# Weighted context of a perceiver layer: fifteen products of thirds of the channels for three blocks of tokens, in place of seven products of halves for two

## The chip, the core and the metric

The kernel runs on one core of one Trainium2 chip. A core has a matrix engine (TensorE, "PE" in the profile; "PEld" is its weight load), a vector engine (VectorE, "DVE"), a scalar engine (ScalarE, "ACT"), GpSimd ("POOL") and a queue engine that only issues transfers ("SP"). The metric is the device time of one execution in microseconds; the median of several runs counts. All data are 32-bit floats.

## The reference, cut to what matters

The layer has three parts: a cross attention of 256 tokens `x` over 25,088 context tokens, a small self attention, and a mixture of experts. The change touches only the cross attention:

```python
# x: 256 x 512 after a layer norm; ctx: 25088 x 512
qp = q @ Wq.T + bq                     # 256 x 128
kp = ctx @ Wk.T + bk                   # 25088 x 128
vp = ctx @ Wv.T + bv                   # 25088 x 512
z = sigmoid(qp @ kp.T / sqrt(128))     # 256 x 25088
x = x + z @ vp
```

There is no softmax, so `z @ vp = (z @ ctx) @ Wv.T + rowsum(z) * bv`. The kernel computes the weighted context `z @ ctx` (256 x 512) first and projects it once at the end.

## The kernel before

**Blocks and groups.** The context is cut into blocks of 128 tokens and groups of J = 4 blocks, so there are G = 49 groups of 512 tokens. For each group four things are done:

1. The keys need the context with channels on the partitions. `turn(g)` (line 313) does this with one VectorE transpose of a second copy of the group ("quarters", loaded by `load_quarters`, line 108, in four transfers of 256 KB); for the first two groups, `turn_by_pe` (line 320) does it on TensorE, 16 transposes each, with copies out of PSUM by ScalarE and VectorE.
2. `keys(g)` (line 339): four matmuls of 512 columns, then a VectorE instruction that adds the bias and moves the result out of PSUM.
3. `scores(g)` (line 360): four matmuls of 256 columns into two PSUM banks, each followed by a ScalarE sigmoid of 512 elements. The result `zT` has 128 tokens on the partitions and, for each block, 256 queries.
4. `values(g)` (line 432): the weighted context. It is a product of a matrix of 2 x 2 pieces (two halves of the queries, two blocks of tokens) and one of 2 x 2 pieces (two blocks of tokens, two halves of the channels). Written out, that is eight products of pieces. The kernel uses the known scheme with seven, which takes sums of pieces as operands: `query_sums` (line 412) makes four sums of `zT` and `context_sums` (line 421) four sums of the context, all on VectorE. The seven products are accumulated over all groups in seven half banks of PSUM (`xacc`), and combined once at the end. A group holds two pairs of blocks, so it makes 14 matmuls of 256 columns.

`summed(g)` (line 384) adds `zT` into `zsum` on VectorE, for the row sums of `z`.

**Order.** Instructions passed to `in_turn` keep their order in the program on their engine. The loop, per group g: loads for g + 2; scores(g); query sums of g; keys(g + 1); channel sums of g + 1; turn(g + 2); summed(g); values(g). TensorE therefore runs scores, keys of the next group, and products, in this order. `in_group` names the groups after which weights of later stages are fetched, each held back by a small GpSimd copy.

**Buffers.** PSUM has eight banks: three in rotation and one apart for keys, scores and transposes (`bank`, line 80), four for the products (`pacc`). In SBUF there are four context groups, three groups of quarters, and two buffers each of turned groups (`cT`), query sums (`S`) and channel sums (`T`); `zT` has three.

**Before the loop:** layer norm of `x`, its transposes, `turn_by_pe(0)`, the query projection, the first keys, `turn_by_pe(1)`. **After the loop:** eight VectorE instructions (lines 501 to 508) combine the seven products into `zc`, `turn_zc` (line 515) turns it in four parts, and the value projection follows (`py`, line 564). The rest of the kernel is the self attention and the experts.

Of the kernel before, what the change touches and what calls it, by code (L numbers as in the profile page):

```python
# [21 lines left out]
def tile_perceiver_layer(  # L22
# [39 lines left out]
    J = 4  # L62
    G = S // (J * P)
    NE = INNER // P
    TOPK = 8

# [10 lines left out]
    psum = ctx.enter_context(tc.tile_pool(name="psum", bufs=3, space=bass.MemoryType.PSUM))  # L77
    turns = [0]

    def bank(name):  # L80
        turns[0] += 1
        return apart(name) if turns[0] % 4 == 0 else among_three(name)

    def among_three(name):
        return psum.tile([P, 512], F32, tag="one", name=name)

    def apart(name):
        return psum.tile([P, 512], F32, tag="apart", name=name, bufs=1)

    pacc = cross.enter_context(tc.tile_pool(name="pacc", bufs=4, space=bass.MemoryType.PSUM))  # L90
# [3 lines left out]
    def load(name, shape, src, pool=const):  # L94
        t = pool.tile(shape, F32, tag=name, name=name, bufs=1)
        nc.sync.dma_start(t, src)
        return t
# [9 lines left out]

    def load_quarters(g):

        q = cpool.tile([P, J * P // R, D // NA], F32, tag="quarters", name=f"quarters_{g}", bufs=3)  # L110
        group = context[g * J * P : (g + 1) * J * P, :]
        for a in range(NA):
            nc.sync.dma_start(
                q[a * R : (a + 1) * R, :, :],
                group.rearrange("(b i) (a d) -> a i b d", i=R, a=NA)[a],
            )
        quarter_tiles[g] = q

    def load_context(g, parts=1):
        t = cpool.tile([P, J, D], F32, tag="ctx", name=f"ctx_{g}", bufs=4)  # L120
        group = context[g * J * P : (g + 1) * J * P, :].rearrange("(j p) d -> p j d", j=J)
        n = J // parts
        for j in range(0, J, n):
            nc.sync.dma_start(t[:, j : j + n, :], group[:, j : j + n, :])
        ctx_tiles[g] = t


    BY_PE = 2
    bk_sb = const.tile([QK, 1], F32, tag="bk", name="bk")
    nc.scalar.dma_start(bk_sb, bk)  # L130
    bq_sb = const.tile([QK, 1], F32, tag="bq", name="bq")
    nc.scalar.dma_start(bq_sb, bq)
    x_sb = act.tile([P, NT, D], F32, tag="x", name="x_sb")
    for t in range(NT):
        nc.sync.dma_start(x_sb[:, t, :], x[t * P : (t + 1) * P, :])
    wqT_sb = load("wqT", [P, ND, QK], rows(wqT))
    load_context(0, parts=J)
    wk_plain_sb = load("wk_plain", [P, ND, QK], rows(wkT), cpool)
    load_context(1)
    wkT_sb = const.tile([P, ND, QK], F32, tag="wkT", name="wkT_sb")  # L140
    for a in range(NA):
        nc.sync.dma_start(
            wkT_sb[a * R : (a + 1) * R, :, :],
            wkT.rearrange("(a c r) e -> a r c e", a=NA, r=R)[a],
        )

# [13 lines left out]
    def all_of(src):  # L160
# [25 lines left out]
        4: [fetch_wv, fetch_bv],  # L186
        6: [fetch_aq],
        8: [fetch_akv, fetch_lng, fetch_lnb],
        10: [fetch_aout],
        12: [fetch_lnog, fetch_lnob, fetch_gates],  # L190
# [42 lines left out]
    idle_sb = cpool.tile([P, 4, 512], F32, tag="T", name="idle_sb")[:, 0, :]  # L233
    nc.vector.memset(idle_sb, 0.0)

    def keep_warm(n):
        pi = bank("pi")
        for _ in range(n):
            nc.tensor.matmul(pi, lhsT=idle_sb[:, 0:P], rhs=idle_sb, start=True, stop=True)
# [60 lines left out]
    def transposed(dst, src, nm):  # L300

        for c in range(ND):
            pt = bank(f"pt_{nm}_{c}")
            for t in range(NT):
                nc.tensor.transpose(
                    pt[:, t * P : (t + 1) * P], src[:, t, c * P : (c + 1) * P], ident
                )
            nc.vector.tensor_copy(dst[:, c, :], pt[:, :T])


    turned_tiles = {}

    def turn(g):

        cT = cpool.tile([P, ND, J * P // R, R], F32, tag="cT", name=f"cT_{g}")
        q = quarter_tiles.pop(g)
        in_turn(nc.vector.transpose(cT, q.rearrange("p b (c r) -> p c b r", r=R)))  # L317
        turned_tiles[g] = cT

    def turn_by_pe(g):  # L320

        cT = cpool.tile([P, ND, J * P // R, R], F32, tag="cT", name=f"cT_{g}")
        ct = ctx_tiles[g]
        for c in range(ND):
            pt = bank(f"ptc_{g}_{c}")
            for j in range(J):
                in_turn(
                    nc.tensor.transpose(
                        pt[:, j * P : (j + 1) * P], ct[:, j, c * P : (c + 1) * P], ident
                    )  # L330
                )
            to = cT[:, c, :, :].rearrange("p b r -> p (b r)")
            if c % 2:
                nc.scalar.copy(to, pt)
            else:
                in_turn(nc.vector.tensor_copy(to, pt))
        turned_tiles[g] = cT

    def keys(g):

        cT = turned_tiles.pop(g)
        pk = bank(f"pk_{g}")
        w = wk_plain_sb if g < BY_PE else wkT_sb
        for c in range(ND):
# [4 lines left out]
                    rhs=cT[:, c, :, :].rearrange("p b r -> p (b r)"),  # L349
# [5 lines left out]
        in_turn(nc.vector.tensor_scalar(kT, pk, bk_sb, None, ALU.add))  # L355
        return kT

    zsum = cpool.tile([P, J, T], F32, tag="zsum", name="zsum", bufs=1)

    def scores(g, kT):  # L360

        zT = cpool.tile([P, J, T], F32, tag="zT", name=f"zT_{g}", bufs=3)
        for h in range(J // 2):
            pz = bank(f"pz_{g}_{h}")
            for i in range(2):
                j = 2 * h + i
                in_turn(
                    nc.tensor.matmul(  # L368
                        pz[:, i * T : (i + 1) * T],
                        lhsT=kT[:, j * P : (j + 1) * P],  # L370
                        rhs=qT,
                        start=True,
                        stop=True,
                    )
                )
            nc.scalar.activation(  # L376
                zT[:, 2 * h : 2 * h + 2, :].rearrange("p j t -> p (j t)"),
                pz,
# [3 lines left out]
        return zT  # L382

    def summed(g, zT):
        if g == 0:
            in_turn(nc.vector.tensor_copy(zsum, zT))
        else:
            in_turn(nc.vector.tensor_add(zsum, zsum, zT))  # L388
# [6 lines left out]
    NP = J // 2  # L395
    HD = D // 2
    product = {}
    for i, names in enumerate((("00", "01"), ("2", "3"), ("1",), ("4", "11"))):
        held = pacc.tile([P, 512], F32, tag="acc", name=f"xacc_{i}")
        for k, nm in enumerate(names):  # L400
            product[nm] = held[:, k * HD : (k + 1) * HD]
    sums, channel_sums = {}, {}

    def z_of(zT, i, b):

        i = 1 - i
        return zT[:, b::2, i * P : (i + 1) * P]

    def c_of(ct, b, k):

        return ct[:, b::2, k * HD : (k + 1) * HD]

    def query_sums(g, zT):
        s = cpool.tile([P, 4, NP, P], F32, tag="S", name=f"S_{g}")
        s1, s2, s3, s4 = (s[:, i, :, :] for i in range(4))
        in_turn(nc.vector.tensor_add(s1, z_of(zT, 1, 0), z_of(zT, 1, 1)))  # L416
        in_turn(nc.vector.tensor_sub(s2, s1, z_of(zT, 0, 0)))
        in_turn(nc.vector.tensor_sub(s3, z_of(zT, 0, 0), z_of(zT, 1, 0)))
        in_turn(nc.vector.tensor_sub(s4, z_of(zT, 0, 1), s2))
        sums[g] = s1, s2, s3, s4  # L420

    def context_sums(g):
        ct = ctx_tiles[g]
        s = cpool.tile([P, 4, NP, HD], F32, tag="T", name=f"T_{g}")
        t1, t2, t3, t4 = (s[:, i, :, :] for i in range(4))
        in_turn(nc.vector.tensor_sub(t1, c_of(ct, 0, 1), c_of(ct, 0, 0)))
        in_turn(nc.vector.tensor_sub(t2, c_of(ct, 1, 1), t1))  # L427
        in_turn(nc.vector.tensor_sub(t3, c_of(ct, 1, 1), c_of(ct, 0, 1)))  # L428
        in_turn(nc.vector.tensor_sub(t4, t2, c_of(ct, 1, 0)))  # L429
        channel_sums[g] = t1, t2, t3, t4  # L430

    def values(g, zT):
        ct = ctx_tiles.pop(g)
        s1, s2, s3, s4 = sums.pop(g)
        t1, t2, t3, t4 = channel_sums.pop(g)
        for nm, lhs, rhs in (
            ("00", z_of(zT, 0, 0), c_of(ct, 0, 0)),
            ("01", z_of(zT, 0, 1), c_of(ct, 1, 0)),
            ("2", s2, t2),
            ("3", s3, t3),  # L440
            ("1", s1, t1),
            ("4", s4, c_of(ct, 1, 1)),
            ("11", z_of(zT, 1, 1), t4),
        ):
            for p in range(NP):

                in_turn(
                    nc.tensor.matmul(  # L448
                        product[nm],
                        lhsT=lhs[:, p, :],  # L450
                        rhs=rhs[:, p, :],
                        start=(g == 0 and p == 0 and nm in ("00", "2", "1", "4")),
# [925 lines left out]
```

## Time and profile before

| | us |
|---|---|
| median of 3 runs | 798.08 (797.95 to 798.08) |
| profiled execution, its own time | 798.27 |
| span of that execution | 796.4 |
| loop: first scores start | 18.02 |
| last product of the loop starts, for a run of 1.03 | 563.21 |
| value projection starts | 565.75 |

A profile shows one execution. For each engine it gives the busy time, and for groups of equal instructions the line of the code, what is written and read, the shape, the count, the busy time, the mean duration of one in ns, and the idle time before them with what ended it. A matmul of 32-bit floats appears as two instructions, so 14 matmuls of the code are 28 in the profile. Matmuls overlap in the engine: the duration of one (380 ns for 256 columns) is longer than the distance between the starts of two. The weight loads' starts show the distance best.

```profile
L346 PE MATMUL pk<-cT,wkT_sb 128*128 128x512 f32 x376 | 169.0, 592 | 0.0
L448 PE MATMUL xacc<-T,S 128*128 128x256 f32 x588 | 134.9, 379 | 0.0
L317 DVE STREAM_TRANSPOSE cT<-quarters 128x2048 f32<-128x2048 f32 x47 | 108.3, 2304 | 0.0
ctx<-in_context SPq DMA_DIRECT2D x48, 1024.0 KB, 6.5
quarters<-in_context SPq DMA_DIRECT2D x188, 256.0 KB, 8.4
```

The first three lines are groups of instructions, the last two transfers (count, size of each, microseconds from issue to landing).

### The profile page before, as it was taken

To read this page: it belongs to the slowest core of one execution; us is meant where nothing else is said; L and a number is where in the kernel's file an instruction comes from. 1 tells how busy PE (TensorE), PEld (TensorE's weight loads), DVE (VectorE), ACT (ScalarE), POOL (GpSimd) and SP (SyncE) were. 2 spreads that over 40 slices of the span, in tenths; PEclk is the share of its full clock that TensorE was granted. 3 is DMA by queue.
4 is the path that set the end of the run, shared out by engine and by line. 5 is a ranking of instruction groups with operands and counts; after the bars stand their busy time and mean duration, and the time that the engine had idled before them with its cause. 6 is when DMAs were issued, how large, how long until landed. Compare 5 with 4: busy or idle time off the path is not lost.

```text
span 796.4 us, 8701 instructions
## 1 busy us (share of the span) xinstructions
PE 784.4 (98%) x3298; PEld 564.5 (71%) x3298; DVE 496.6 (62%) x820; ACT 112.3 (14%) x248; POOL 21.4 (3%) x44
## 2 busy tenths in 40 slices
PE   9999999999999999999999999999999899999996
PEld 5777777777777777777777777777676586776563
DVE  5766776677766776677766776676656563512222
ACT  2111101110011101110011101110245220110110
POOL 1000000000000000000000000000223000000000
PEclk9999999999999999999999999999999999999998
DMA  9967998999887778777887778720510042769400
GB/s 279 257 165 185 258 243 242 244 248 242 200 205 185 174 176 209 191 184 170 197 206 184 174 177 211 193 72 0 196 44 1 1 133 96 252 233 392 163 1 30
DMA packets 150497, 139.59 MB, mean 175 GB/s; under 512 B 7984, under 2 KB 109872, under 8 KB 150448
## 3 DMA queue, kind: packets, MB, share of 16 engines
q1 hardware_dynamic: 150160, 138.96, 67.1%
q8 instruction: 28, 0.46, 0.3%
q14 instruction: 21, 0.17, 0.1%
q10 hardware_dynamic: 288, 0.00, 0.0%
HBM read 138.42 MB, written 0.52 MB: 174 GB/s over the span
## 4 chain that ended last, share of the span: by engine, by line
PE 96%; DVE 2%; ACT 1%; DMA 0%; POOL 0%; issue 0%; ACTq 0%
PE xacc L448 37%; PE pk L346 21%; PE pz L368 11%; PE ph_e L936 7%; PE pd_e L983 3%; PE ph_s L936 3%; PE pd_s L983 2%; PE pa L651 2%; PE ph_few L1205 1%; PE pw L715 1%; PE py L564 1%; PE ps L741 1%; PE ptp L792 1%; PE po_few L1236 1%; PE pf L1182 1%; PE pd_few L1250 1%
## 5 line engine op out<-in xcount | busy, mean ns | idle before, releaser
L346 PE MATMUL pk<-cT,wkT_sb 128*128 128x512 f32 x376 | 169.0, 592 | 0.0
L448 PE MATMUL xacc<-T,S 128*128 128x256 f32 x588 | 134.9, 379 | 0.0
L376 ACT ACTIVATE zT<-pz 128x512 f32<-128x512 f32 x98 | 58.3, 597 | 479.9 <-PE pz L368 479.2
L448 PEld LDWEIGHTS xacc<-T,S 128*128 128x128 f32 x588 | 111.7, 190 | 15.2
L346 PEld LDWEIGHTS pk<-cT,wkT_sb 128*128 128x128 f32 x376 | 71.4, 190 | 69.9 <-issue 67.4
L317 DVE STREAM_TRANSPOSE cT<-quarters 128x2048 f32<-128x2048 f32 x47 | 108.3, 2304 | 0.0
L448 PEld LDWEIGHTS xacc<-ctx,zT 128*128 128x128 f32 x392 | 74.3, 190 | 31.3 <-issue 23.0
L448 PE MATMUL xacc<-ctx,zT 128*128 128x256 f32 x392 | 93.0, 380 | 0.1
L368 PE MATMUL pz<-qT,kT 128*128 128x256 f32 x392 | 92.6, 379 | 0.0
L368 PEld LDWEIGHTS pz<-qT,kT 128*128 128x128 f32 x392 | 74.4, 190 | 10.1
L416 DVE TENSOR_TENSOR S<-zT 128x256 f32<-128x256 f32 x49 | 20.8, 425 | 91.4 <-ACT zT L376 91.4
L355 DVE TENSOR_SCALAR kT<-pk,bk 128x512 f32<-128x512 f32 x49 | 36.8, 751 | 59.8 <-PE pk L346 59.8
L936 PE MATMUL ph_e<-fT,gu 128*128 128x256 f32 x256 | 57.4, 381 | 0.0
L388 DVE TENSOR_TENSOR zsum<-zsum,zT 128x1024 f32<-128x1024 f32 x48 | 56.8, 1184 | 0.0
L936 PEld LDWEIGHTS ph_e<-fT,gu 128*128 128x128 f32 x256 | 48.0, 190 | 10.6 <-issue 2.2
L448 PE MATMUL xacc<-T,zT 128*128 128x256 f32 x196 | 50.3, 379 | 0.0
L448 PE MATMUL xacc<-ctx,S 128*128 128x256 f32 x196 | 50.3, 379 | 0.0
L448 PEld LDWEIGHTS xacc<-T,zT 128*128 128x128 f32 x196 | 37.2, 190 | 5.1
L448 PEld LDWEIGHTS xacc<-ctx,S 128*128 128x128 f32 x196 | 37.2, 190 | 5.1
L427 DVE TENSOR_TENSOR T<-ctx,T 128x512 f32<-128x512 f32 x49 | 33.9, 692 | 1.7
L428 DVE TENSOR_TENSOR T<-ctx 128x512 f32<-128x512 f32 x49 | 33.5, 685 | 0.0
L429 DVE TENSOR_TENSOR T<-T,ctx 128x512 f32<-128x512 f32 x49 | 33.5, 684 | 0.0
(231 smaller groups left out, 611.3 us busy)
## 6 DMA issues: line engine op xcount, KB each, us to landing
ctx<-in_context SPq DMA_DIRECT2D x48, 1024.0 KB, 6.5
quarters<-in_context SPq DMA_DIRECT2D x188, 256.0 KB, 8.4
gu<-in_e_gate_up SPq DMA_DIRECT2D x12, 1024.0 KB, 7.5
dn<-in_e_down SPq DMA_DIRECT2D x11, 512.0 KB, 4.7
gu_s<-in_s_gate_up SPq DMA_DIRECT2D x8, 512.0 KB, 5.9
a_wqT<-in_a_wqT SPq DMA_DIRECT2D x1, 2048.0 KB, 8.8
a_wout<-in_a_woutT SPq DMA_DIRECT2D x1, 2048.0 KB, 9.9
dn_s<-in_s_down SPq DMA_DIRECT2D x4, 512.0 KB, 7.2
```

Source lines behind the costliest of these rows:

```text
L317: in_turn(nc.vector.transpose(cT, q.rearrange("p b (c r) -> p c b r", r=R)))
L346: nc.tensor.matmul(pk, lhsT=w[:, c, :], rhs=cT[:, c, :, :].rearrange("p b r -> p (b r)"), start=(c == 0), stop=(c == ND - 1),)
L355: in_turn(nc.vector.tensor_scalar(kT, pk, bk_sb, None, ALU.add))
L368: nc.tensor.matmul(pz[:, i * T : (i + 1) * T], lhsT=kT[:, j * P : (j + 1) * P], rhs=qT, start=True, stop=True,)
L376: nc.scalar.activation(zT[:, 2 * h : 2 * h + 2, :].rearrange("p j t -> p (j t)"), pz, AF.Sigmoid, scale=1.0 / math.sqrt(QK),)
L388: in_turn(nc.vector.tensor_add(zsum, zsum, zT))
L427: in_turn(nc.vector.tensor_sub(t2, c_of(ct, 1, 1), t1))
L428: in_turn(nc.vector.tensor_sub(t3, c_of(ct, 1, 1), c_of(ct, 0, 1)))
L429: in_turn(nc.vector.tensor_sub(t4, t2, c_of(ct, 1, 0)))
L448: nc.tensor.matmul(product[nm], lhsT=lhs[:, p, :], rhs=rhs[:, p, :], start=(g == 0 and p == 0 and nm in ("00", "2", "1", "4")), stop=(g == ...
L936: nc.tensor.matmul(ph[:, f * T + lo : f * T + hi], lhsT=gu[:, c, col : col + P], rhs=fT[:, c, lo:hi], start=(c == 0), stop=(c == ND - 1),)
L983: nc.tensor.matmul(pd, lhsT=hT[:, f, t * P : (t + 1) * P], rhs=dn[:, f, :], start=(f == 0), stop=(f == NI - 1),)
```

## The change

- **Groups of three blocks.** J is 3. 25,088 tokens are 65 groups of 384 and one block over; that block becomes group 0 (`blocks_of`, `tokens_of`), and is the only one turned by TensorE (four transposes).
- **Fifteen products.** The pieces are now two halves of the queries by three blocks of tokens, and three blocks of tokens by three thirds of the channels. Written out, that is 18 products; the change uses a scheme with fifteen. 512 channels do not divide by three, so the thirds are 170 to 172 wide and overlap. `a02` is the first half of the queries with the third block, `b21` the third block with the second third, `s` are sums of a's, `t` sums of b's, `p` the products. Ten query sums of 128 elements are made by VectorE; of thirteen channel sums of 172 elements six by VectorE and seven by GpSimd. The products fill six PSUM banks. In the first group, which has only its middle block, three sums and six products are left.
- **Banks.** Keys and scores have one bank each (`keys_bank`, `scores_bank`), the products six. The scores of a group come in two parts, of two blocks and of one, through the same bank.
- **Order.** The products run one group late: scores of two blocks of g; four products of g - 1; scores of the third block; keys(g + 1); the other eleven products of g - 1. VectorE: channel sums of g, query sums of g, turn(g + 2). GpSimd: channel sums of g, then `summed(g)`. Loads are issued three groups ahead, with five context buffers.
- **Engines.** The bias of the keys is added by ScalarE, `zsum` by GpSimd.
- **Start.** The two halves of `x` are loaded on two queues, the query weights on ScalarE's queue, the biases on GpSimd's; the two layer norms are interleaved; three pairs of warming matmuls in place of four.
- **End.** ScalarE copies five of the six product banks to SBUF, 21 sums on VectorE and GpSimd combine them, `zc` is turned in two parts, the second between the matmuls of the first projection.

```diff
-    J = 4
-    G = S // (J * P)
+    J = 3
+    HEAD = S % (J * P)
+    G = 1 + S // (J * P)
...
-    pacc = cross.enter_context(tc.tile_pool(name="pacc", bufs=4, space=bass.MemoryType.PSUM))
+    psum = ctx.enter_context(tc.tile_pool(name="psum", bufs=1, space=bass.MemoryType.PSUM))
+    pacc = cross.enter_context(tc.tile_pool(name="pacc", bufs=6, space=bass.MemoryType.PSUM))
...
     def keys(g):
...
-        in_turn(nc.vector.tensor_scalar(kT, pk, bk_sb, None, ALU.add))
+        in_turn(nc.scalar.activation(kT[:, 0:n], pk, AF.Identity, bias=bk_sb))
...
     def summed(g, zT):
+        part = slice(blocks_of(g)[0], blocks_of(g)[-1] + 1)
+        in_turn(nc.gpsimd.tensor_add(zsum[:, part, :], zsum[:, part, :], zT[:, part, :]))
...
+    WIDTH = 172
+    third_at = (0, 340, 170)
+    S_SUMS = """
+        s0 a02 + a12
+        s1 s0 - a00
+        s2 a01 + s0
+        s3 a10 - s1
+        s4 a11 + s2
+        s5 a11 - s3
+        s6 s4 - a10
+        s7 a00 - a02
+        s8 a01 + s5
+        s9 a01 + a02
+    """
+    T_SUMS = """
+        t0 b01 + b21
+        t2 b00 + t0
+        t7 b00 + b01
+        t11 b02 - t0
+        t12 b11 + t7
+        t8 t2 + t4
+    """
+    T_SUMS_BY_POOL = """
+        t1 b10 + b12
+        t3 t1 - b22
+        t4 b20 - t3
+        t9 b02 + t1
+        t5 b12 - b22
+        t10 t5 - b11
+        t6 b11 - b02
+    """
+    PRODUCTS = (
+        ("p6 s2 t3", "p14 s0 t8", "p8 s5 b11"),
+        ("p13 s6 b02", "p11 s8 t6"),
+        ("p5 a12 b20", "p1 a01 t10", "p7 s1 t2"),
+        ("p0 s9 b22", "p9 a00 t11"),
+        ("p10 a10 b00", "p4 s7 b21"),
+        ("p12 s4 t9", "p3 a11 b10", "p2 s3 t12"),
+    )
...
+    RESULTS = """
+        u6 p6 + p14
+        u0 p13 - p8
...
+        u3 p2 + p4
+        u11 p12 - p0
+        | u7 p8 + u3
+        u5 p3 + p13
+        u10 p3 + p5
+        | u14 u11 - p6
+        c10 p10 + u10
+        c11 u7 + u8
+        | c12 u14 - u5
+    """
+    WIDE = ("p2", "p4", "p7", "p8", "p9", "p10", "p11", "p13")
...
+    def do_sums(engine, text, named):
+        for line in text.strip().splitlines():
+            to, x_, op, y_ = line.split()
+            f = engine.tensor_add if op == "+" else engine.tensor_sub
+            in_turn(f(named[to], named[x_], named[y_]))
...
     for g in range(G):
...
+        context_sums(g, named)
+        blocks = blocks_of(g)
+        scores(g, kT, zT, blocks[0:2])
+        if before is not None:
+            values(before, 0, 4)
+        if len(blocks) > 2:
+            scores(g, kT, zT, blocks[2:3])
+        if g + 1 < G:
+            kT = keys(g + 1)
+        if before is not None:
+            values(before, 4)
+        query_sums(g, named)
+        if g + 2 < G:
+            turn(g + 2)
+        summed(g, zT)
...
+    values(before)
...
+    for i in range(len(PRODUCTS) - 1):
+        n = max(cols.stop for b, cols in product.values() if b == i)
+        in_turn(nc.scalar.copy(held[i][:, 0:n], banks_of_products[i][:, 0:n]))
...
+    project_values(0, range(0, 2))
+    turn_zc(1, sum_bank)
+    project_values(0, range(2, ND))
...
+    project_values(1, range(ND))
```

A line of `RESULTS` that begins with a bar is done by GpSimd, the others by VectorE.

## The prediction

> **What bounds the kernel now.** I read the page first (busy shares, the 40 slices, the chain of waits), then the windows of three groups in the middle, then the timeline of one group, then the groups by form for prices.
>
> ```profile
> PE 784.4 (98%) x3298; PEld 564.5 (71%) x3298; DVE 496.6 (62%) x820; ACT 112.3 (14%) x248; POOL 21.4 (3%) x44
> PE 96%; DVE 2%; ACT 1%; DMA 0%; POOL 0%; issue 0%; ACTq 0%
> ...
> 300.00:311.20 11.20, 11.20 (x45) 8.36 (x45) 8.10 (x11) 1.19 (x2) 0.00 (x0) 1.00 0.81 194
> 311.20:322.40 11.20, 11.20 (x45) 8.36 (x45) 8.09 (x11) 1.20 (x2) 0.00 (x0) 1.00 0.83 184
> ```
>
> TensorE carries 96% of the chain. In the windows (columns: length, then busy time of PE, PEld, DVE, ACT, POOL, then clock, DMA share, GB/s) it has no idle time in a group of 512 tokens, which takes 11.20 us at full clock. So the 49 groups, 548.8 us, are bought in TensorE time alone, and one must ask what TensorE streams per token. The starts of the weight loads give the spacing of passes (each f32 matmul of the code appears twice):
>
> ```profile
> 311.46 0.19 PEld L346 LDWEIGHTS pk<-cT,wkT_sb 128*128 128x128 f32 x1 [0.24 <-issue]
> 311.89 0.19 PEld L346 LDWEIGHTS pk<-cT,wkT_sb 128*128 128x128 f32 x1 [0.24 <-issue]
> 312.32 0.19 PEld L346 LDWEIGHTS pk<-cT,wkT_sb 128*128 128x128 f32 x1 [0.24 <-issue]
> ...
> 315.98 2.56 PEld L448 LDWEIGHTS xacc<-T,S 128*128 128x128 f32 x12
> ...
> 579.50 0.97 PEld L683 LDWEIGHTS pv<-a_wkv,anT 128*128 128x128 f32 x8
> ...
> 631.17 3.65 PEld L936 LDWEIGHTS ph_first<-fT,gu_s 128*128 128x128 f32 x32
> ```
>
> 512 columns: 0.43 us a pass. 256 columns: (2.56 - 0.19)/11 = 0.215. 128 columns: (3.65 - 0.19)/31 = 0.112; 64 columns, (0.97 - 0.19)/7 = 0.111, cost no less, so 0.111 is the floor that the weight load sets. Between 128 and 512 columns a pass costs 0.84 ns a column. Sum of a group now: 8 passes of 512 and 36 of 256, 8 x 0.43 + 36 x 0.215 = 11.18: the measured 11.20.
>
> **What the Trainium skill says.** "TensorE: Matmul & The Clock Gate", LDWEIGHTS, has a load cost columns/1.2 ns, 107 ns for 128; the trace's floor of 111 ns agrees. It matters because the new passes (172 columns) come near it. "GPSIMD Engine Reference", Performance versus the Vector engine, gives about 2.6 cycles an element with two inputs; the trace agrees (below). "SBUF — State Buffer", Who interferes with whom, says that a VectorE instruction with two SBUF inputs contends with a GpSimd instruction that reads SBUF, and that the loser is fully blocked. No pair of that kind overlaps here (POOL is idle in all groups), so this is my open cost.
>
> **The change part by part.**
>
> *TensorE in the loop.* At 0.84 ns a column: 384 columns 0.3225 us, 172 columns 0.1444, 170 columns 0.1428, all above the floor of 0.111. A group of 384 tokens: keys 8 x 0.3225 = 2.58; scores 6 x 0.215 = 1.29; fifteen products, 16 passes of 172 (2.31) and 14 of 170 (2.00). Sum 8.18 us. 65 groups make 531.7; the single first block adds keys 8 x 0.112 = 0.89, scores 0.43 and six products 12 x 0.1435 = 1.72, so 3.0. Total 534.7 against 548.8: **-14.1 us**. Per token the products fall from 11.8 to 11.2 ns and the rest stays, which is why so little comes of it.
>
> *Before the loop.* The last product of before ends at 564.24, so 564.24 - 548.8 = 15.4 us lie ahead of or between loop work. After: only one block is turned by TensorE (4 transposes for 32, which cost 3.9 us), x comes on two queues, and the first group's keys wait for quarters. In the first 20 us the DMA is the limit (share 0.97, 279 GB/s, about 310 after the first 2 us). Up to the first quarters 2.1 MB are asked for, which land at about 9.5 us; turning 1.7 gives 11.3, qT 11.8, scores(0) and keys(1) end at 15, kT(1) 15.75, then scores(1) 0.86, four products 1.16, scores 0.43, keys(2) (its quarters at 15.5, turned 17.3) 2.58, two products 0.57: group 2 starts at about 21.3. From there 64 turns of 8.18, less one keys (2.58) plus the last products (4.31), give 546.6; with the last pass's tail (0.16) 546.8. That is 17.4 us before 564.24, of which 3.3 are from the start.
>
> *After the loop.* Before, 1.5 us pass from the last product to the first value projection:
>
> ```profile
> 563.21 1.03 PE L448 MATMUL xacc<-T,zT 128*128 128x256 f32 x4
> 565.75 7.13 PE L564 MATMUL py<-wvT,zcT 128*128 128x512 f32 x16 [0.17 <-ACT zcT L528]
> ```
>
> After, 5 bank copies by ACT (0.59 each for 512) and most of the 21 sums lie under the last products, since a bank's products are issued together. Behind the last product stay u3, u11, u5, u10, c10 (0.25 each, from the DVE price below), a POOL sum, c11, c12; the first half of zc is ready about 1.0 us after the last product, its transposes take 0.43, its copy 0.59, and the projection starts about 2.4 us after; the second half's transposes (0.43) sit inside the projection. 2.4 + 0.43 - 1.5 = **+1.4 us**. Everything later is the same work in the same order.
>
> *VectorE, POOL, ACT in the loop.*
>
> ```profile
> 300.66 0.43 DVE L416 TENSOR_TENSOR S<-zT 128x256 f32<-128x256 f32 x1 [1.79 <-ACT zT L376]
> 301.12 0.42 DVE L417 TENSOR_TENSOR S<-S,zT 128x256 f32<-128x256 f32 x1
> 301.46 0.42 DVE L418 TENSOR_TENSOR S<-zT 128x256 f32<-128x256 f32 x1
> ...
> 305.46 0.69 DVE L428 TENSOR_TENSOR T<-ctx 128x512 f32<-128x512 f32 x1
> 306.06 0.68 DVE L429 TENSOR_TENSOR T<-T,ctx 128x512 f32<-128x512 f32 x1
> 306.66 2.30 DVE L317 STREAM_TRANSPOSE cT<-quarters 128x2048 f32<-128x2048 f32 x1
> 308.89 1.18 DVE L388 TENSOR_TENSOR zsum<-zsum,zT 128x1024 f32<-128x1024 f32 x1
> ...
> L512 POOL TENSOR_TENSOR zsum<-zsum 128x512 f32<-128x512 f32 x1 | 1.3, 1273 | 406.5 <-DVE zsum L388 406.5
> L513 POOL TENSOR_TENSOR zsum<-zsum 128x256 f32<-128x256 f32 x1 | 0.7, 728 | 0.1
> ```
>
> Start to start, a VectorE sum takes 0.60 for 512 and 0.34 for 256 (0.12 more if it needs its predecessor): 1.04 ns an element, so 0.21 for 128 and 0.25 for 172. Ten query sums 2.2, six channel sums 1.65, one turn of 1,536 elements (2.23 x 3/4) 1.7: 5.5 us of 8.18. POOL: 728 and 1273 give 2.13 ns an element plus 183 ns, so 172 elements 0.55 and 768 elements 1.82; seven sums and zsum 5.66 us. ACT: sigmoids 0.60 and about 0.4, key bias 0.48. Each alone fits, hidden by TensorE. In the order of the changed kernel POOL's sums of a group wait until the T buffer of two groups back is free, so they start with the group and end at 3.8 us; zsum follows. VectorE's query sums start when the second sigmoid is done, about 3.2 us in, and the turn after them is due 2.5 us into the next group (keys stand third there), so VectorE has some 3.5 us of slack in order and 2.7 in throughput.
>
> *New waits on TensorE.* One bank serves both parts of the scores. Streaming of the first part ends, 0.26 us later ACT starts (in the trace the first four passes, from 309.30, end at 310.16 and ACT starts at 310.42), 0.60 for the sigmoid: 0.86, under four products (8 passes, 1.15 us). Cover 0.29 us. If it is gone, everything behind on TensorE waits; 0.1 us a group would cost 6.5.
>
> *DMA.* 1.57 MB per 8.18 us is 192 GB/s against 187 now, at a share near 0.8 and loaded a group earlier; taken as nothing. If the DMA were late by 0.1 us a group it would be the same 6.5.
>
> *The open cost.* If VectorE's two-input sums and POOL's instructions exclude each other, the need of the shared port per group lies between 6.6 us (elements alone: 2,312 x 1.04 ns and 1,972 x 2.13 ns) and 9.5 us (3.85 + 5.66 in full). The group is 8.18. A gain is excluded, since exclusion speeds nothing up. I take zero stall, because POOL's seven sums fall partly under the turn (one input) and the middle of the bounds, 8.05, still fits; the end 9.5 is kept.
>
> **Sum.** -14.1 - 3.3 + 1.4 = -16.0. The profiled execution took 798.27 (span 796.4 and 1.9 around it), 0.2 over the median 798.08; so 782.3 as profiled, **782 us** for the median.
>
> **Rivals.**
> 1. *TensorE paces, but with small stalls* (single scores bank, late T8 or keys): 0.1 to 0.2 us a group, 6.5 to 13 us: about 790. For it: the cover of 0.29 is thin, and more handovers per us. Against: before runs without a gap under the same kinds of waits.
> 2. *The port decides, slower than before.* VectorE's sums wait behind POOL's, the turn comes late, and keys wait for it in each group. It becomes slower than before above 8.18 + 16/65 = 8.43 us a group. At 9.0: +53 - 16, about 835; at 9.5, about 868. For it: both engines were idle from each other until now, and zsum (1.8 us) meets the query sums. Against: it needs nearly full holding of the port, as computed.
> 3. *Nothing in sum*: stalls of 0.25 us a group eat the gain, about 798.
>
> **Chances.** Forecast 0.53 (own range 777 to 788), rival 1 0.17 (788 to 796), rival 3 0.04, rival 2 0.26. A measurement of this kernel tells about 0.2% (1.6 us) from no change. Faster 0.69, same 0.04, slower 0.27. The range 777 to 822: below it lies little, above it the worse two thirds of rival 2, about 0.16.
>
> **What would show it.** Right: a period of 8.2 us per group in the windows, PE busy throughout, keys starting without a wait on VectorE, POOL's 172-element sums near 0.55 us. Passes of 172 at 0.19 us would prove the floor of the weight load wrong (+90 us). Rival 2 would show as VectorE sums far over 0.3 us or POOL's over 0.55 where both run, and "keys wait for cT" on TensorE. Rival 1 would show idle time before the second scores. The start is right if the second full group begins near 21 us, the end if the projection starts 2.4 us after the last product.

## The result, and the profile after

| | before | after |
|---|---|---|
| median of 7 runs, us | 798.04 (797.76 to 798.17) | 795.74 (793.15 to 796.75) |
| profiled execution, us | 798.27 | 796.75 |
| its span | 796.4 | 794.9 |
| last product ends | 564.24 | 561.21 |
| value projection starts | 565.75 | 563.61 |

The ratio is 0.9965, with a 95% interval of 0.995 to 0.9979: the change makes the kernel faster by 2.3 us, 0.3%. The direction is the forecast one, and the time lies in the range; but the forecast was a gain of 16 us, and a seventh of it came. This section shows where the other 14 went. It reads the profiled execution, which is the slowest of the seven and 1 us above their median.

The page of the kernel after, engine shares and the chain of waits:

```profile
PE 775.6 (98%) x3994; PEld 609.6 (77%) x3994; DVE 636.8 (80%) x1389; ACT 157.8 (20%) x350; POOL 400.1 (50%) x574
...
DVE 52%; PE 40%; DMA 3%; issue 2%; POOL 1%; ACT 1%; SPq 0%; DVEq 0%; POOLq 0%; ACTq 0%
```

TensorE is as full as before (98%), and yet more than half of the chain now runs over VectorE, where it was 96% TensorE. Two engines are close to their limit together. The window of one group (length, then busy time of PE, PEld, DVE, ACT, POOL, then granted clock, DMA share, GB/s) says how close:

```profile
300.00:308.20 8.20, 8.20 (x46) 6.93 (x45) 8.13 (x19) 1.56 (x3) 5.74 (x8) 1.00 0.82 190
```

TensorE has no idle time here, so it still paces the loop; but VectorE, for which the prediction had added up 5.5 us of work, is busy for 8.13. The timeline of VectorE and GpSimd in the same group shows what fills it (start, duration, engine; the last line is TensorE's):

```profile
303.70 0.55 POOL L501 TENSOR_TENSOR T<-T,ctx 128x172 f32<-128x172 f32 x1
303.75 0.70 DVE L501 TENSOR_TENSOR T<-ctx 128x172 f32<-128x172 f32 x1
...
304.37 2.49 DVE L501 TENSOR_TENSOR T<-ctx,T 128x172 f32<-128x172 f32 x2
304.76 1.91 POOL L379 TENSOR_TENSOR zsum<-zsum,zT 128x768 f32<-128x768 f32 x1
306.78 0.33 DVE L501 TENSOR_TENSOR T<-T 128x172 f32<-128x172 f32 x1
...
308.92 0.68 POOL L501 TENSOR_TENSOR T<-ctx 128x172 f32<-128x172 f32 x1 [2.25 <-PE xacc L527]
...
309.17 1.77 DVE L315 STREAM_TRANSPOSE cT<-quarters 128x1536 f32<-128x1536 f32 x1
...
311.13 2.74 PE L339 MATMUL pk<-cT,wkT_sb 128*128 128x384 f32 x8
```

A sum of 172 elements takes VectorE 0.33 us when GpSimd is idle (306.78), 0.70 beside a GpSimd sum of 0.55 (303.75), and two of them take 2.49 us when `zsum` (1.91 us) falls on them: they end 0.19 us after it. VectorE waits while GpSimd reads, and the trace books the wait as busy time. The turn of the context then ends at 310.94, and the keys that need it start at 311.13. In the loop VectorE is therefore in time, by 0.2 us. GpSimd itself waits 2.25 us in each group for TensorE to give a buffer of channel sums back; this may be what keeps the two engines from running further into one another, but no run tests it.

So the loop is not where most of the time is lost. TensorE's timeline at the start of the loop is (scores are `pz`, keys `pk`):

```profile
13.92 1.19 PE L360 MATMUL pz<-qT,kT 128*128 128x256 f32 x2 [2.83 <-DVE qT L575]
14.90 5.31 PE L339 MATMUL pk<-cT,wkT_sb 128*128 128x384 f32 x8
20.88 1.13 PE L360 MATMUL pz<-qT,kT 128*128 128x256 f32 x4 [0.67 <-ACT kT L348]
...
26.91 1.13 PE L360 MATMUL pz<-qT,kT 128*128 128x256 f32 x4 [0.15 <-ACT kT L348]
...
30.47 2.85 PE L339 MATMUL pk<-cT,wkT_sb 128*128 128x384 f32 x8 [0.84 <-DVE cT L315]
```

The first scores come late, the keys of group 1 take 5.31 us where the same eight passes take 2.74 later on, and the keys of group 3 wait for VectorE's turn. And at the last products, where no scores and keys lie between them any more:

```profile
551.86 1.85 POOL L379 TENSOR_TENSOR zsum<-zsum,zT 128x768 f32<-128x768 f32 x1
...
551.97 3.02 DVE L501 TENSOR_TENSOR S<-zT,S 128x128 f32<-128x128 f32 x4
...
554.00 0.81 PE L527 MATMUL xacc<-T,S 128*128 128x170 f32 x4 [0.95 <-DVE S L501]
...
555.78 0.81 PE L527 MATMUL xacc<-ctx,S 128*128 128x172 f32 x2 [0.17 <-DVE S L501]
```

Four query sums, 0.89 us in the loop, take 3.02 beside `zsum`; the products of the last group need them and wait. From about 556 to 559.25 a pass takes 0.28 us instead of 0.145: the granted clock is 0.50 there. From these views and the rest of TensorE's timeline, the sum against the prediction:

| stretch | predicted | measured | more by |
|---|---|---|---|
| until group 2 starts | 21.3 | 26.91 | 5.6 |
| group 2 | 8.18 | 9.44 (26.91 to 36.35) | 1.3 |
| the 62 groups from 3 to 64 | 8.18 each | 8.24 each (36.35 to 547.25) | 3.7 |
| from the last scores to the end of the last product | 10.1 | 14.0 (547.25 to 561.21) | 3.9 |
| from there to the self attention, against before | +1.4 | +1.3 | -0.1 |

14.4 us in all; -16.0 + 14.4 = -1.6, and the profiled execution is 1.5 us faster than that of before. The largest single term is the start, the rest comes from group 2, the ends, and a small amount in each group.

### The profile page after: what moved, and what is told of

It is laid out like the page before. It is cut to its first block, busy times and chain, and to the rows that moved or that the text cites. A ratio compares the mean times of both kernels' runs of the same rounds, so it can differ in the third digit from the quotient of the medians.

```text
span 794.9 us, 11690 instructions
## 1 busy us (share of the span) xinstructions
PE 775.6 (98%) x3994; PEld 609.6 (77%) x3994; DVE 636.8 (80%) x1389; ACT 157.8 (20%) x350; POOL 400.1 (50%) x574
## 4 chain that ended last, share of the span: by engine, by line
DVE 52%; PE 40%; DMA 3%; issue 2%; POOL 1%; ACT 1%; SPq 0%; DVEq 0%; POOLq 0%; ACTq 0%
DVE T L501 27%; DVE S L501 13%; DVE cT L315 11%; PE xacc L527 7%; PE ph_e L1089 7%; PE pk L339 5%; PE pd_e L1136 3%; DMA quarters<-in_context 3%; PE ph_s L1089 3%; PE pz L360 2%; PE pd_s L1136 2%; PE pa L804 2%; PE ph_few L1358 1%; PE pw L868 1%; PE py L690 1%
## 5 line engine op out<-in xcount | busy, mean ns | idle before, releaser
L501 POOL TENSOR_TENSOR T<-ctx 128x172 f32<-128x172 f32 x195 | 124.0, 636 | 143.7 <-PE xacc L527 143.7
L501 DVE TENSOR_TENSOR T<-ctx,T 128x172 f32<-128x172 f32 x195 | 190.6, 1003 | 2.2
L339 PE MATMUL pk<-cT,wkT_sb 128*128 128x384 f32 x520 | 181.3, 492 | 0.9 <-DVE cT L315 0.8
L527 PE MATMUL xacc<-T,S 128*128 128x170 f32 (+1 forms) x782 | 167.4, 309 | 0.9 <-DVE S L501 0.9
L379 POOL TENSOR_TENSOR zsum<-zsum,zT 128x768 f32<-128x768 f32 (+1 forms) x66 | 123.9, 1877 | 14.4 <-ACT zT L369 14.4
L315 DVE STREAM_TRANSPOSE cT<-quarters 128x1536 f32<-128x1536 f32 x65 | 115.1, 1771 | 5.8 <-DMA quarters<-in_context 5.8
L527 PE MATMUL xacc<-ctx,S 128*128 128x172 f32 (+1 forms) x522 | 108.9, 310 | 0.4 <-DVE S L501 0.4
L527 PE MATMUL xacc<-ctx,zT 128*128 128x170 f32 (+1 forms) x394 | 89.5, 309 | 0.0
L501 DVE TENSOR_TENSOR T<-ctx 128x172 f32<-128x172 f32 x132 | 81.5, 618 | 0.0
L501 DVE TENSOR_TENSOR S<-zT,S 128x128 f32<-128x128 f32 x325 | 78.8, 292 | 0.0
L501 POOL TENSOR_TENSOR T<-T,ctx 128x172 f32<-128x172 f32 x130 | 67.5, 519 | 10.2
```

The lines of the kernel that those rows point to most:

```text
L315: in_turn(nc.vector.transpose(new_turned(g), q.rearrange("p b (c r) -> p c b r", r=R)))
L339: nc.tensor.matmul(pk, lhsT=w[:, c, :], rhs=cT[:, c, 0 : n // R, :].rearrange("p b r -> p (b r)"), start=(c == 0), stop=(c == ND - 1),)
L379: in_turn(nc.gpsimd.tensor_add(zsum[:, part, :], zsum[:, part, :], zT[:, part, :]))
L501: in_turn(f(named[to], named[x_], named[y_]))
L527: nc.tensor.matmul(banks_of_products[i][:, cols], lhsT=named[lhs], rhs=named[rhs][:, 0 : cols.stop - cols.start],  start=i not in opened, ...
```

## The experiments

Two theories were set against each other first. *The start*: the late quarters and a TensorE at half clock (granted clock 0.50 from 14 to 20 us) cost the most, and warming it gets that back. *The port*: VectorE runs late because GpSimd's reads hold it, which is free in the loop and paid for where the loop begins and ends. Every time below is beside the kernel before in the same batch (798.05 for the first four, 798.17 for the others).

**e1_warm: the start alone.** Three matmuls on idle data bridge TensorE's wait for the query.

```diff
+    pi = keys_bank("pi_late")
+    for _ in range(3):
+        in_turn(nc.tensor.matmul(pi, lhsT=idle_sb[:, 0:P], rhs=idle_sb, start=True, stop=True))
     turn(1)
```

> Three 512-column matmuls on idle data are put between the query projection and the first scores, where TensorE idles 2.8 us and then runs at half clock. Theory start (half clock is part of the missing gain): keys of group 1 take about 2.6 us in place of 5.3, group 2 starts 2 to 3 us earlier, time about 793.2 against 795.7. Rival transfers (the start is bound by the loads, so an earlier TensorE only waits later): group 2 or 3 waits that much longer, time unchanged, 795 to 796.

Measured: 794.35 (793.39 to 795.45), ratio 0.9951 (0.9938 to 0.9965). TensorE's timeline:

```profile
14.42 2.74 PE L339 MATMUL pk<-cT,wkT_sb 128*128 128x384 f32 x8
...
29.20 2.85 PE L339 MATMUL pk<-cT,wkT_sb 128*128 128x384 f32 x8 [2.02 <-DVE cT L315]
...
35.07 1.03 PE L360 MATMUL pz<-qT,kT 128*128 128x256 f32 x4
```

The keys of group 1 take 2.74 us, and the scores of group 1 come 3.0 us earlier (17.84 against 20.88). But the keys of group 3 now wait 2.02 us for VectorE where they waited 0.84, and the scores of group 3 are only 1.3 us earlier (35.07 against 36.35). TensorE got faster and met VectorE's delay: in this trace the clock's cost is real, and VectorE's delay takes more than half of the gain back. The median is 1.4 us below that of the kernel after, less than the runs of either differ among themselves.

**e2_zsum_on_vector: the port alone.** The largest of GpSimd's reads goes to VectorE, which by the prediction's addition has the time.

```diff
-        in_turn(nc.gpsimd.tensor_add(zsum[:, part, :], zsum[:, part, :], zT[:, part, :]))
+        in_turn(nc.vector.tensor_add(zsum[:, part, :], zsum[:, part, :], zT[:, part, :]))
```

> The 768-element zsum addition of each group moves from GpSimd to VectorE. Theory port (VectorE's sums stand still while GpSimd reads two operands; VectorE's lag costs nothing within the loop but is paid in the first groups and at the last products): VectorE's busy time per group falls from 8.13 to about 7.4 us although it gets 0.9 us more to do, the period stays 8.23, the last fifteen products take about 5 us in place of 8.15, time about 791.5. Rival own work (VectorE is full with its own instructions, no exclusion): 8.13 + 0.87 = 9.0 us a group, which sets the pace, time about 846.

Measured: 788.68 (788.5 to 789.58), ratio 0.9886 (0.9871 to 0.9901), 7.1 us below the median of the kernel after. The group of VectorE's dependent channel sums, the scores of group 3, and the window of one group:

```profile
L501 DVE TENSOR_TENSOR T<-ctx,T 128x172 f32<-128x172 f32 x195 | 121.7, 649 | 2.2
...
32.08 1.03 PE L360 MATMUL pz<-qT,kT 128*128 128x256 f32 x4
...
300.00:308.23 8.23, 8.23 (x46) 7.01 (x45) 8.16 (x19) 1.56 (x3) 4.37 (x8) 1.00 0.83 205
```

The mean of these sums was 1,003 ns in the kernel after; it is 649 now, since none stands behind a 1.9 us read. The period is 8.23, as it was: in the loop nothing was to be gained. What changed are the ends. The scores of group 3 start at 32.08 (36.35 after), with no wait of the keys for VectorE, and the last products take 4.36 us (8.15 after) without a wait. VectorE is also less late within the loop: in the group from 300 us on its turn ends 1.8 us before the keys that need it (304.35 against 306.17), where the kernel after had 0.2. VectorE's busy time did not fall, against the expectation: it has 0.98 us more to do and meets more of GpSimd's short sums, whose waits count as busy. In this execution the keys of group 1 took 2.74 us without any extra matmuls, so a part of its gain at the start is the clock's, which differs between executions.

**e3_zsum_last_on_vector: the end alone.** The same move for the last group only.

```diff
+        engine = nc.vector if g == G - 1 else nc.gpsimd
+        in_turn(engine.tensor_add(zsum[:, part, :], zsum[:, part, :], zT[:, part, :]))
```

> Only the last group's zsum addition moves from GpSimd to VectorE, behind its query sums. Theory port: the loop is unchanged (8.23 a group), and the last fifteen products take about 6 us in place of 8.15, time about 793.7. Rival: the stall at the last products comes from the order of VectorE's own sums; no change, 795.7.

Measured: 792.38 (791.16 to 793.58), ratio 0.9934 (0.992 to 0.9947): 3.4 us below the kernel after, by one instruction of 66. There is no wait at the last products, and the period stays 8.23. From the last scores to the end of the last product it takes 10.2 us (14.0 after, 10.1 predicted): this is nearly all of the 3.9 us of the table's fourth line.

**e4_warm_zsum_on_vector: both edits, of e1 and e2.**

> Both of the first two edits. If the start and the lag are separate terms their gains add: about 2.5 + 4 us less than 795.7, so 789. If they hide each other, as much as the larger one alone, 791 to 792.

Measured: 789.14 (788.78 to 789.38), ratio 0.9889 (0.9874 to 0.9904). The time is near the expected one, but not because the two gains add: e2 alone reaches 788.68. Once VectorE is in time, warming adds nothing that can be measured. Against e1, which has the same warm start, the move of `zsum` is worth 5.2 us, so the gain of e2 is not an accident of the clock at the start. Why e2 needs no warming, the runs don't show; only one of its four was profiled.

**e5_all_sums_on_vector: GpSimd out of the loop.** To e2's edit is added that the seven channel sums go to VectorE, so nothing holds the port.

```diff
-            do_sums(nc.gpsimd, T_SUMS_BY_POOL, named)
+            do_sums(nc.vector, T_SUMS_BY_POOL, named)
```

> GpSimd does nothing in the loop: all 13 channel sums, the 10 query sums and zsum are VectorE's. Theory port: without a reader beside it no VectorE sum of 172 elements is over 0.35 us (0.57 to 0.62 now in half of them), and VectorE's own need is 2.14 (query sums) + 1.7 (turn) + 0.9 (zsum) + 13 x 0.25 with some dependent ones, about 3.6: 8.35 us a group, just over TensorE's 8.23; time 790 to 800. Rival own work (the sums are slow by themselves, as at 0.6 us now): 13 x 0.6 + 4.7 = 12.5 us a group, time above 1,050.

Measured: 802.73 (801.86 to 804.8), ratio 1.0061 (1.0045 to 1.0076): slower than before, and 2.7 us above the end of the expected range. A group of VectorE's sums, and TensorE's weight loads for the keys of one group (each group near it has a line of this form):

```profile
L501 DVE TENSOR_TENSOR T<-ctx,T 128x172 f32<-128x172 f32 x325 | 97.6, 333 | 4.5
...
313.34 2.23 PEld L339 LDWEIGHTS pk<-cT,wkT_sb 128*128 128x128 f32 x8 [0.29 <-DVE cT L315]
```

All of VectorE's sums of 172 elements are now 0.32 to 0.34 us, so GpSimd alone had lengthened them; but VectorE's own work now sets the period, 8.39 us (8.35 was expected), and the keys wait for it in each of these groups. Of the 14 us above e2 this is 10; in its profiled execution the rest lies in group 2, at the last products and in value projections at half clock. Sharing the sums is right, in spite of the port; how they are shared is the question.

**e8_pool_writes_only: is it reading, or any work of GpSimd?** In place of `zsum`'s addition GpSimd writes the same tile twice, so the row sums are left out.

```diff
-        in_turn(nc.gpsimd.tensor_add(zsum[:, part, :], zsum[:, part, :], zT[:, part, :]))
+        for _ in range(2):
+            in_turn(nc.gpsimd.memset(zsum, 0.0))
```

> The zsum addition on GpSimd is replaced by two memsets of the same tile, which write and read nothing (the row sums are left out, so the bias term of the output is missing). Theory port for readers only: VectorE's sums beside them are not held; no VectorE sum of over 1 us remains (2.2 us under zsum now), the last products take about 5 us, time about 789. Rival (any GpSimd instruction holds VectorE's two-input sums): sums of over 1 us remain, as long as the memset.

Measured: 789.42 (788.14 to 791.46), ratio 0.9892 (0.9879 to 0.9906). The timeline of both engines in one group:

```profile
300.41 0.55 POOL L502 TENSOR_TENSOR T<-T,ctx 128x172 f32<-128x172 f32 x1
300.45 0.66 DVE L502 TENSOR_TENSOR S<-zT 128x128 f32<-128x128 f32 x1
...
301.40 1.53 POOL L380 MEMSET zsum<- 128x768 f32 x2
301.53 0.88 DVE L502 TENSOR_TENSOR S<-zT,S 128x128 f32<-128x128 f32 x4
```

Beside the writes four query sums take 0.88 us together, their free duration; beside a GpSimd sum (300.41) one alone takes 0.66. Of the two kinds of GpSimd instructions in this loop only the sums, which read, hold VectorE, and the gain of e2 comes from taking away the reading, not from taking away GpSimd's work or adding to VectorE's.

**e6_group1_by_tensor: the rest of the start.** To e2's edit is added that group 1, too, is turned by TensorE out of its context tile (twelve transposes), so that its quarters are not loaded and VectorE's first turn falls away.

```diff
-    load_quarters(1)
+    load_context(1)
...
-        w = wkT_sb if g > 0 else wk_plain_sb
+        w = wkT_sb if g > 1 else wk_plain_sb
...
-    turn(1)
...
+    turn_group_by_pe(1)
```

> On top of zsum on VectorE (788.7): group 1 is turned by TensorE again, from its context tile; its quarters (0.79 MB) aren't loaded, and the turned key weights aren't needed before group 2. Theory start (TensorE waits 2.9 us for the first quarters and their turn): scores of group 0 no longer wait for the quarters, group 2 starts about 2 us earlier (21.7 in place of 23.75), time about 787. Rival: the load of the context tile or the 12 transposes and 4 copies take as long as the quarters did, 788.7 or more.

Measured: 788.37 (786.84 to 788.86), ratio 0.9871 (0.9856 to 0.9886). The first scores start at 12.56 without a wait (13.92 after, 13.80 in e2), the scores of group 2 at 22.45 (23.75 in e2). Of these 1.3 us the median keeps 0.3, which is less than the runs of e6 differ from each other: inconclusive for the time, clear for the wait. The profiled execution shows one place where the gain went: its last product ends 1.2 us earlier than in e2, but the granted clock is 0.50 from 556 to 558 us, and the first four passes of the value projection, together with the transposes behind them, take 3.6 us (2.3 in e2).

**e7_start_end_zsum: a version from these findings.** e6, and the 21 closing sums all on VectorE, without the handovers to GpSimd.

```diff
-        engine = nc.gpsimd if "|" in line else nc.vector
+        engine = nc.vector
```

> As the run with group 1 turned by TensorE, and all 21 closing sums are VectorE's. If the closing sums lose time by the exchange with GpSimd (0.55 us each there, 0.25 on VectorE, and blocking), the projection starts about 0.4 us earlier after the last product (2.76 now), time 0.4 us below that run. Rival: VectorE becomes the longer chain and it is no faster.

Measured: 786.85 (785.87 to 788.14), ratio 0.9863 (0.9848 to 0.9878): 11.3 us below the kernel before and 8.9 below the median of the kernel after. Its median is the lowest of all, though its runs overlap those of e6. The projection starts 2.69 us after the last product (2.97 in e6, 2.76 in e2), so the closing sums account for 0.1 to 0.3 us of it, where 0.4 was expected. Of the 3.6 us that its profiled execution (785.92) stands above the forecast 782.3, some 3 are the 63 periods of 8.23 in place of 8.18.

## Why the prediction was right in direction and wrong in size

- *TensorE in the loop, -14.1 us: right in kind, 3.7 us too good over the 62 groups from 3 to 64.* The loop is paced by TensorE and the weight load does not bind. The mis-sized term is the price of a pass. I took 0.84 ns a column, which is 0.43 us by 512 and 0.215 by 256, and so a price without a fixed part. In the trace of after, the weight loads of seven products (14 passes) lie between these two starts:

```profile
306.21 0.33 PEld L527 LDWEIGHTS xacc<-T,S 128*128 128x128 f32 x2
...
308.24 0.33 PEld L527 LDWEIGHTS xacc<-T,S 128*128 128x128 f32 x2
```

  2.03 / 14 = 0.145 us for 171 columns on average, against 0.1436. With it the group is 2.58 + 1.29 + 30 x 0.145 = 8.22, within 0.01 of the measured window, so no stall is needed to explain it. The points 256 (0.215), 384 (0.3225) and 512 (0.43) lie on one line with it, of about 0.835 ns a column and some 2 ns more for each pass. The price explains 2.6 of the 3.7 us; the other 0.02 us a group were not traced.
- *The start, -3.3 us: wrong, it cost 2.3.* Two steps failed here. The quarters of group 1 were expected at 9.5 us and the turn began at 11.62, so the first scores were 2.1 late: I had taken about 310 GB/s after the first 2 us, and the transfers moved 225 to 290 until then. The wait of 2.83 us that this made on TensorE was followed by half clock, which the sum had at nothing: 2.6 us in the keys of group 1 and 0.5 in the scores before them. The remaining 0.4 lie between the scores of group 1 and of group 2. The Trainium skill, "TensorE: Matmul & The Clock Gate", Part 1: The HAM clock gate, says that the clock halves after an idle window of about 3.4 us, and that the windows' phase differs between runs. The runs here agree in the halving and in the difference between executions: these keys take 2.74, 4.28 and 5.31 us in kernels that share this start (e2, e3, after). They do not agree in the length: the clock fell during or right after waits of 2.83 (after) and 2.32 us (e3), shorter than the page's window, and stayed full after one of 2.91 (e2).
- *The open cost, taken as zero: beside the start, this is the step that failed.* The prediction saw the exclusion between VectorE's sums and GpSimd's, named the section of the skill on it, and bounded its need inside a steady group. There zero was right (8.23 with `zsum` on either engine). What it left out is that a delay which fits into a period still exists as a delay, and shows wherever the period's cover is missing: 1.3 us in group 2, where VectorE starts with nothing done ahead, and 3.9 us at the last products, where neither scores nor keys lie between the last sums and their use. Of these 3.9 some 2.4 are waits and 1.5 are passes at half clock after them: in e1, whose clock stays full there, the same stretch takes 12.5 us (546.38 to 558.87), 2.4 more than predicted. That the waits bring the clock down was not tested apart. e3 (3.4 us back by one instruction) shows the second; e1 (1.7 of 3.0 us lost again) and e2 (no wait in group 2) show the first, and e4 against e1 (5.2 us) shows both together.
- *VectorE 5.5 us a group: the work was priced right, its time was not.* A sum of 172 elements that needs no predecessor takes 0.25 us from start to start in e5 (0.33 in duration) and the turn 1.77, against 0.25 and 1.7 predicted; waiting makes 8.13 of it. Rival 2, a port that decides every group, was the right mechanism in the wrong place; its 8.43 us a group was never reached. That the buffers which TensorE gives back limit the overlap is a guess.
- *Small stalls from the single bank of scores (rival 1): not seen.* TensorE's passes fill 8.22 of the 8.23 us. That the time, 795.74, lies in the range of this rival is chance.
- *The end, +1.4 us: right,* 1.3; the projection starts 2.4 us after the last product, as written. The parts named in the working (1.0, 0.43 and 0.59) come to 2.0; the 0.4 that it adds without naming is what the handovers took (1.06 to the transposes, 0.70 to the copy, 0.64 to the projection).
- *Two slips of the working change nothing:* 1.04 ns a VectorE element is 1.02 by the starts that it shows (0.60 less 0.34, for 256), and its times up to the last product add up to 546.7, not 546.8.

Not settled: why the clock falls in some executions and not in others, why the transfers at the start were slower than taken, and the 1 us that the start of e6 still stands behind the predicted one (22.45 against 21.3). None of these was tried further.

## What to carry to other kernels

Slack that a second engine spends in a steady loop is owed once at each end of it: after adding up a period, walk through the first and the last group with the same delays, where nothing covers them. Of two engines that share a port, give the long reading reduction to the engine that loses anyway, since one long read under its sums costs more than doing the work there. A price per column that is taken from long passes alone leaves out what each pass costs besides its columns, and shorter passes pay that more often.

## What the runs showed of the hardware

- VectorE's two-input sums stand still while GpSimd reads, for as long as that instruction lasts: 0.33 us becomes 0.70 beside 0.55, and up to 2.3 beside 1.9. This is what the Trainium skill, "SBUF — State Buffer", Who interferes with whom, says; not expected was that VectorE was the one that paid most, while GpSimd's sums stayed nearer their own time (0.49 to 0.68 in the loop, 0.48 to 0.55 at the start, where VectorE runs no sum beside them). GpSimd's memset held nothing, and VectorE's turn, which has one input, was not held: 1.77 us beside GpSimd's sums (309.17) and in e5 without any.
- A held VectorE counts as busy: 8.16 of 8.23 us with `zsum` on GpSimd and on VectorE alike, though the second has 0.98 us more work. Busy time of an engine that shares a port isn't its work.
